# A recurrent cell on one core: one PSUM copy of the odd groups placed ahead of two state copies, split weights made in steps 12 to 19, and DMA waits placed in front of the last store

## The chip, the cores and the metric

The kernel runs on one core of one Trainium2 chip. The metric is the device time of one execution in microseconds (us); the median of three runs of the kernel before is 1650.72 us. The core has five instruction streams that wait for each other through semaphores: TensorE (PE, with its weight loads listed as PEld), VectorE (DVE), ScalarE (ACT), GpSimd (POOL) and SyncE (SP), which issues most DMAs.

## What is computed

x has 8 sequences of 512 steps with 512 features, and h starts from `cond_1024` (8 x 512). Each step needs the state of the step before, so nothing can run ahead along time except the products with x.

```python
def step(h, x_t):
    fused = sigmoid(concatenate([x_t, h], -1) @ w_W + w_b)
    hidden_state, output_state = split(fused, 2, -1)          # r and z
    memory_state = x_t @ wx_W + wx_b + hidden_state * (h @ wh_W + wh_b)
    h_new = output_state * h + (1.0 - output_state) * tanh(memory_state)
    return h_new, h_new
x = x + hs                                                     # hs: all h_new, batch first
```

## The kernel before

**Steps and groups.** The main loop (L615) runs over i = 0 to 511, one time step each. Four steps make a group; eight steps make an octet `o`, and `u` is the step's place in it (L722). Groups with `u` 0 to 3 are called even here, those with `u` 4 to 7 odd. The x side of a whole group is computed ahead, in pieces: behind its own matmuls on h, each step does a share of the products of x for a later group (`x_step`, 384 columns in steps with u 0 to 3 and 288 in the others, L48), and these matmuls write the tiles `xp` and `eps`.

**One step.** The matmuls on h go to three outputs: A (192 columns), B (128) and C (64), in the order of `ORDER` (L26): A0 B0 A1 A2 A3 B1 B2 B3 C0 to C3, where the digit is the quarter of h. C holds the second half of the gate z and lies in the PSUM bank `cs`. DVE transposes the outputs, ACT does sigmoid and tanh, and DVE scans (`m`, then `hT`) make the new state; `hT` of the first half, written by `update(0, 0)` (L726), is what A0 of the next step waits for.

**C in two forms.** In steps where `in_parts(i)` holds (L492: even groups from step 8 on), C is made of bf16 parts: POOL splits h into three parts (`split`, L751 to 761), and 48 bf16 matmuls use the weights `wb`, `w2` and `w3` (`parts`, L434). In the others it is made of 16 f32 matmuls. An f32 matmul of the code stands in the trace as two, so the trace counts 32 where the code has 16. `w2` and `w3` are made by POOL in steps 1 to 4, four operations of 128x128 a step (L762 to 770).

**The x side goes into PSUM ahead of the matmuls.** For an odd group `spread(2 * o + 1, ...)` copies the pieces A, B and C of `odd` into the PSUM banks with ACT: A and C in step u = 1, B in step u = 2 (L795 to 804). C of an odd group lands in the bank `cs`, in which the even group's C is still being made. `spread_c` (L495, four copies with a mask) does it for C of an even group, two in step 6 and two in step 7 (L749).

**ACT around step u = 1.** At a step's end ACT copies the new state into its other slot, a copy for each half (L751). Then, in step u = 1, it copies `eps` to `more` (only for 0 < o < 62, L776 and 797), then `spread` A and C. The next work in its queue is the sigmoid of the next step (`md0A<-tr`).

**What sets the order.** Each engine works through its instructions in the order in which the code adds them. `Flow.plan` (L132) puts a wait in front of an instruction for each operand that another engine still reads or writes; a PSUM bank counts as a whole (L179 to 184), so a matmul into `cs` waits for the last ACT copy into `cs` that the code added before it.

**The end.** In step 511 DVE adds the last half of the output (L855), SP issues the last store (L856), and then SP waits for the semaphores of all 24 DMA lanes (L251 to 253).

Of the kernel before, what the change touches and what calls it, by code (L numbers as in the profile page):

```python
# [11 lines left out]
ALU = mybir.AluOpType  # L12
# [3 lines left out]
NQ = 4  # L16
GS = 4
HS = 12
B = 8
HU = 64  # L20
# [4 lines left out]
IDLE = 3  # L25
# [61 lines left out]
class Flow:  # L87
# [146 lines left out]
    def emit(self, tc):  # L234

        self.plan()
        sems = {e: tc.alloc_semaphore(f"flow_{e}") for e in self.ENGINES}
        lanes = [tc.alloc_semaphore(f"flow_dma{n}") for n in range(self.LANES)]
        count = {}
        with tc.tile_critical():  # L240
            for item in self.items:
                engine = getattr(self.nc, item.engine)
                for other in sorted(item.waits, key=lambda o: o.index):
                    engine.wait_ge(other.sem, other.value)
                inst = getattr(self, item.op, getattr(engine, item.op, None))(*item.args, **item.kw)  # L245
                if item.lane is not None or item.signal:
                    sem, by = (lanes[item.lane], 16) if item.lane is not None else (sems[item.engine], 1)
                    count[sem.name] = count.get(sem.name, 0) + by
                    item.sem, item.value = sem, count[sem.name]
                    inst.then_inc(sem, by)  # L250
            for sem in lanes:  # L251
                if sem.name in count:
                    self.nc.sync.wait_ge(sem, count[sem.name])


@with_exitstack
def tile_cond_rnn_residual(
# [40 lines left out]
    nc = Flow(tc.nc)  # L298
    NCH = x.shape[0]
    T = NCH * TC  # L300
    NG = T // GS
    LAST = NG // 2 - 1
# [56 lines left out]
    wb = const.tile([P, NQ, NQ, 192], F32, name="wb")  # L359
# [13 lines left out]
    NH = 2 * GS  # L373
# [3 lines left out]
    w2 = const.tile([P, NQ, NQ, HU], F32, name="w2")  # L377
    w3 = const.tile([P, NQ, NQ, HU], F32, name="w3")
# [35 lines left out]
    def state(hf, i, slot=2):  # L414

        s = i % GS
        return hT[hf][i % NH][:, B * s : B * s + B, :, slot]
# [13 lines left out]
    def high(t_):  # L431
        return t_.bitcast(BF16)
# [29 lines left out]
    def act(out_, in_, func, **kw):  # L462
        return nc.scalar.activation(out_, in_, func, **kw)
# [10 lines left out]
    def keep(g):  # L474

        nc.vector.tensor_tensor(
            source(g)[:, XC], (piece if g == 2 else xps[g % 2])[:, XC], bias[:, XC], ALU.add
        )

    def source(g):  # L480

        return xps[g % 2] if g // 2 == LAST else (even, odd)[g % 2]

    def spread(g, names):

        for n in names:
            nc.scalar.copy(banks[g % 2][n], source(g)[:, XP[n]])

    def cell(i):
        return cs[:, HU * (i % GS) : HU * (i % GS) + HU] if i // GS % 2 == 0 else banks[1]["C"]  # L490

    def in_parts(i):  # L492
        return NH <= i < T and i // GS % 2 == 0

    def spread_c(g, steps_):  # L495

        for s in steps_:
            nc.scalar.activation(
                cell(GS * g + s), source(g)[:, XP["C"]], AF.Copy, scale=mask[:, s, :1]
            )  # L500

    def turn_x(g, hf):

        c0 = XP["X"].start + HU * hf
        nc.vector.transpose(
            md1[hf][g % 2][:, :, :, 1].rearrange("p n c -> p c n"), source(g)[:, c0 : c0 + HU]
        )

    def reg(r, c=XC):
        return xps[r[0]][r[1], c]  # L510
# [18 lines left out]
    def x_sum(o, n):  # L529

        t_ = [q[o % 2] for q in sx]
        a, b, op = [
            (x_half(o, 1, 0), x_half(o, 1, 1), ALU.add),
            (t_[0], x_half(o, 0, 0), ALU.subtract),
            (x_half(o, 0, 0), x_half(o, 1, 0), ALU.subtract),
            (x_half(o, 0, 1), t_[1], ALU.subtract),
        ][n]
        nc.gpsimd.tensor_tensor(t_[n], a, b, op)
# [76 lines left out]
    for i in range(T):  # L615
# [8 lines left out]
        for n in (ORDER if i else FIRST).split():  # L624
# [3 lines left out]
            bank, k = n[0], int(n[1])  # L628
            lhsT = hs[i % NH][:, k, :32, 2]
            for j in range(NQ):  # L630
                if bank == "C" and in_parts(i):
                    parts(cell(i)[32 * j : 32 * j + 24], i, k, j)
                else:
                    to = cell(i) if bank == "C" else ps[bank]
# [8 lines left out]
        def scan(c_, out_, d0, d1):  # L643

            return nc.vector.tensor_tensor_scan(
                *[t_[:, :, c_].rearrange("p n c s -> p (n c s)") for t_ in (out_, d0, d1)],
                0.0,
                ALU.mult,
                ALU.add,
            ).ins  # L650
# [59 lines left out]
        def update(hf, q):  # L710
            s1 = (i + 1) % GS
            new = hT[hf][(i + 1) % NH][:, B * s1 : B * s1 + B]
            return scan(slice(q, q + 1), new, hd0[hf][i % 2], hT[hf][i % NH][:, rows])
# [8 lines left out]
        o, u = divmod(i, 2 * GS)  # L722
# [22 lines left out]
            memory(1, 1)  # L745
        update(1, 0)
        update(1, 1)
        if nxt and u in (6, 7):
            spread_c(2 * o + 2, (2 * u - 12, 2 * u - 11))  # L749
        for hf in range(2):  # L750
            act(state(hf, i + 1, 0), state(hf, i + 1), AF.Copy)  # L751
            if in_parts(i + 1):
                ks, s1 = slice(2 * hf, 2 * hf + 2), B * ((i + 1) % GS)
                t_, new = split[(i + 1) % 2][:, ks], hs[(i + 1) % NH][:, ks]
                nc.gpsimd.tensor_tensor(
                    t_[:, :, :2].rearrange("p k u b -> p k b u"),
                    new[:, :, s1 : s1 + B, 2].unsqueeze(3).broadcast_to([P, 2, B, 2]),
                    high(new).rearrange("p k (u n) s -> p k n u s", u=2)[:, :, s1 : s1 + B, :, 5],
                    ALU.subtract,
                )  # L760
                nc.gpsimd.tensor_tensor(t_[:, :, 2], t_[:, :, 0], high(t_)[:, :, 0, 1::2], ALU.subtract)
        if 1 <= i <= NQ:  # L762
            for n in range(0, NQ, 2):
                for to, t_ in ((w2, wb[:, :, :, :HU]), (w3, w2)):
                    nc.gpsimd.tensor_tensor(
                        to[:, i - 1, n : n + 2],
                        t_[:, i - 1, n : n + 2],
                        high(t_)[:, i - 1, n : n + 2, 1::2],
                        ALU.subtract,
                    )  # L770
        if i < 3:
            inst = load_x(i + 1)
            if i == 0:
# [5 lines left out]
        if o == LAST:  # L779
            if u == 2:  # L780
                spread(2 * o + 1, "AB")
                turn_x(2 * o + 1, 0)
                turn_x(2 * o + 1, 1)
            elif u == 3:
                spread(2 * o + 1, "C")
        elif u == 0:
            if o == 0:
                spread(1, "A")
            if sums:
                nc.scalar.copy(reg(BE), reg(AL))  # L790
                nc.scalar.copy(both[LO], reg(DE))
                x_sum(o + 1, 3)
            turn_x(2 * o + 1, 0)
            turn_x(2 * o + 1, 1)
        elif u == 1:  # L795
            if sums:
                nc.scalar.copy(more[HI], eps)
            spread(2 * o + 1, "BC" if o == 0 else "AC")
        elif u == 2:
            if sums:  # L800
                nc.vector.tensor_tensor(reg(GA), reg(BE), more[HI], ALU.add)
                nc.scalar.copy(even[LO, XC], reg(AL))
            if o:
                spread(2 * o + 1, "B")
        elif u == 3:
            if sums:
                nc.vector.tensor_tensor(odd[HI, XC], reg(GA), both[LO], ALU.add)
                nc.scalar.copy(both[HI], reg(DE))
            if two:
                x_sum(o + 2, 2)  # L810
        elif u == 4:
            if o == 0:
                keep(3)
            if two:
                nc.scalar.copy(reg(AL), bias[LO, XC])
                x_sum(o + 2, 0)
        elif u == 5:
            if sums:
                nc.vector.tensor_tensor(even[HI, XC], reg(BE), both[HI], ALU.add)
            if two:  # L820
                nc.scalar.copy(reg(DE), step_bias[HI])
        elif u == 6 and nxt:
            spread(2 * o + 2, "AB")
            turn_x(2 * o + 2, 0)
        elif u == 7 and nxt:
            if o:
                nc.scalar.copy(odd[LO, XC], reg(GA))
            turn_x(2 * o + 2, 1)
            if two:
                x_sum(o + 2, 1)  # L830
        if 1 <= i < 9:
            weight_sum(1 if i < 5 else 3, *divmod((i - 1) % 4, 2))
        if i == 2:
            nc.scalar.copy(step_bias[HI], bias[LO, XC])
            nc.gpsimd.tensor_tensor(step_bias[HI], bias[HI, XC], step_bias[HI], ALU.subtract)
        for n in range(IDLE - 1):
            nc.vector.memset(idle[:, n : n + 1], 0.0)
        def add(hf, engine):
            return engine.tensor_tensor(
# [98 lines left out]
```

## Time and profile before

| | |
|---|---|
| three runs, us | 1650.20, 1650.72, 1652.10 |
| the profiled execution: its time, us | 1651.85 |
| its span, first to last instruction, us | 1649.9 |
| granted TensorE clock, mean | 0.999 |
| DVE busy, us | 1241.6 (75%) |
| ACT busy, us | 1256.4 (76%) |
| POOL busy, us | 542.0 (33%) |

The profile has one row for a group of like instructions: the start, the time that they took together, the engine, the line, the operation, what it writes and reads, how many, and in brackets how long the engine sat idle before and what ended that. Nearly all instructions carry the line of the helper that issues them (L245), so groups are told apart by the names of the tiles. A busy PE is no proof that PE is at its peak: the ends of matmuls are modelled, and a matmul that is held up can hide behind the tail of the one before.

### The profile page before, as it was taken

To read this page: it belongs to the slowest core of one execution; us is meant where nothing else is said; L and a number is where in the kernel's file an instruction comes from. 1 tells how busy PE (TensorE), PEld (TensorE's weight loads), DVE (VectorE), ACT (ScalarE), POOL (GpSimd) and SP (SyncE) were. 2 spreads that over 40 slices of the span, in tenths; PEclk is the share of its full clock that TensorE was granted. 3 is DMA by queue.
4 is the path that set the end of the run, shared out by engine and by line. 5 is a ranking of instruction groups with operands and counts; after the bars stand their busy time and mean duration, and the time that the engine had idled before them with its cause. 6 is when DMAs were issued, how large, how long until landed. Compare 5 with 4: busy or idle time off the path is not lost.

```text
span 1649.9 us, 127364 instructions
## 1 busy us (share of the span) xinstructions
PE 1637.8 (99%) x58330; PEld 1394.7 (85%) x50266; DVE 1241.6 (75%) x9443; ACT 1256.4 (76%) x6190; POOL 542.0 (33%) x2304
## 2 busy tenths in 40 slices
PE   8999999999999999999999999999999999999998
PEld 5888888888888888888888888888888888888887
DVE  7777777777777777777777777777777777777776
ACT  4777777777777777777777777777777777777775
POOL 3323323333233233333332333333333333333332
PEclk9999999999999999999999999999999999999999
DMA  4000000000000000000000000000000000000000
GB/s 183 12 15 17 15 15 16 16 15 15 15 17 15 15 15 18 14 15 15 17 15 15 15 18 14 15 15 18 15 14 15 18 15 14 15 18 10 10 10 11
DMA packets 37298, 31.26 MB, mean 19 GB/s; under 512 B 4084, under 2 KB 35060, under 8 KB 36600
## 3 DMA queue, kind: packets, MB, share of 16 engines
q1 hardware_dynamic: 36576, 22.89, 4.5%
q8 instruction: 425, 6.96, 1.7%
q14 instruction: 145, 1.19, 0.2%
q10 hardware_dynamic: 152, 0.22, 0.1%
HBM read 14.70 MB, written 8.39 MB: 14 GB/s over the span
## 4 chain that ended last, share of the span: by engine, by line
PE 98%; DVE 1%; ACT 0%; issue 0%; DVEq 0%; SPq 0%
PE A L245 41%; PE B L245 27%; PE xp L245 17%; PE cs L245 9%; PE cs L219 4%; PE eps L245 1%; DVE m L245 0%; DVE tr L245 0%; DVE tw L245 0%; DVE hT L245 0%; DVE md1A L245 0%; DVE tz L245 0%; DVE md1B L245 0%; DVE even L245 0%; ACT cs L245 0%
## 5 line engine op out<-in xcount | busy, mean ns | idle before, releaser
L245 PE MATMUL A<-wa,hT 128*32 128x192 f32 x16384 | 872.5, 327 | 3.7 <-DVE hT L245 3.7
L245 PEld LDWEIGHTS A<-wa,hT 128*32 128x32 f32 x16384 | 547.9, 122 | 192.8 <-DVE hT L245 134.0
L245 PE MATMUL B<-wb,hT 128*32 128x128 f32 x16384 | 653.1, 273 | 0.0
L245 PEld LDWEIGHTS B<-wb,hT 128*32 128x32 f32 x16384 | 542.8, 122 | 21.2 <-DMA wb<-in_wb_dram 0.9
L245 POOL TENSOR_TENSOR ot<-xin,hT 128x16 f32<-128x16 f32 x991 | 225.4, 252 | 594.4 <-DVE hT L245 592.5
L245 ACT ACTIVATE hT<-m 128x8 f32<-128x8 f32 x2048 | 350.5, 208 | 77.9 <-DVE m L245 68.1
L245 DVE STREAM_TRANSPOSE tr<-A 128x64 f32<-128x64 f32 x512 | 128.2, 250 | 290.1 <-PE A L245 284.0
L245 POOL TENSOR_TENSOR split<-hT 128x32 f32<-128x32 f32 x504 | 131.3, 261 | 432.1 <-DVE m L245 420.3
L245 PE MATMUL xp<-tw,sx 128*32 128x384 f32 (+2 forms) x1464 | 263.4, 433 | 0.0
L245 ACT ACTIVATE hT<-hT 128x16 f32<-128x16 f32 x1024 | 217.0, 225 | 60.3 <-DVE hT L245 57.7
L245 DVE TENSOR_TENSOR_SCAN hT<-hd0B,hT 128x24 f32<-128x24 f32 x1024 | 180.9, 205 | 74.7 <-ACT hT L245 50.7
L245 ACT ACTIVATE md0A<-tr 128x16 f32<-128x16 f32 x512 | 112.2, 219 | 158.1 <-DVE tr L245 156.6
L245 PE MATMUL xp<-wx,xin 128*32 128x384 f32 (+4 forms) x1348 | 220.8, 413 | 0.0
L245 DVE TENSOR_TENSOR_SCAN hT<-hd0A,hT 128x24 f32<-128x24 f32 x1024 | 199.0, 194 | 0.0
L245 PE MATMUL cs<-wb,hT 128*32 128x64 f32 x8320 | 169.3, 219 | 0.0
L245 PEld LDWEIGHTS cs<-wb,hT 128*32 128x32 f32 x8320 | 157.6, 122 | 0.4 <-issue 0.3
L245 DVE TENSOR_TENSOR_SCAN m<-md0A,md1A 128x16 f32<-128x16 f32 x1024 | 143.1, 182 | 16.2 <-ACT md0A L245 8.1
L245 DVE TENSOR_TENSOR_SCAN m<-md0B,md1B 128x16 f32<-128x16 f32 x1024 | 145.6, 163 | 0.8 <-DVE tzB L245 0.4
L219 PE MATMUL cs<-w,split 128*24 128x64 bf16 x8064 | 135.2, 192 | 0.6 <-issue 0.6
L245 ACT ACTIVATE hd0A<-tz 128x16 f32<-128x16 f32 x512 | 115.1, 225 | 18.3
L245 PE MATMUL cs<-wb,split 128*24 128x64 bf16 x4032 | 127.2, 193 | 0.3 <-issue 0.2
L245 PEld LDWEIGHTS cs<-wb,split 128*24 128x24 bf16 x4032 | 108.2, 92 | 21.5 <-issue 12.6
(101 smaller groups left out, 2223.1 us busy)
## 6 DMA issues: line engine op xcount, KB each, us to landing
out_dram<-ot SPq DMA_DIRECT2D x128, 64.0 KB, 1.6
xin<-in_x_dram SPq DMA_DIRECT2D x112, 64.0 KB, 2.4
wx<-in_wx_dram SPq DMA_DIRECT2D x4, 768.0 KB, 7.0
wa<-in_wa_dram SPq DMA_DIRECT2D x4, 384.0 KB, 9.7
wb<-in_wb_dram SPq DMA_DIRECT2D x1, 1152.0 KB, 13.5
xin<-in_x_dram SPq DMA_DIRECT2D x3, 256.0 KB, 3.5
wb<-in_wb_dram SPq DMA_DIRECT2D x1, 384.0 KB, 13.9
head<-in_xh_dram ACTq DMA_DIRECT2D x1, 208.0 KB, 4.7
```

The costliest lines, as they stand in the source:

```text
L219: return t.add_instruction(mybir.InstMatmult(name=self.nc.get_next_instruction_name(), ins=[t.lower_ap(rhs), t.lower_ap(lhsT)], outs=[t.lo ...
L245: inst = getattr(self, item.op, getattr(engine, item.op, None))(*item.args, **item.kw)
```

## The change

- `spread(2 * o + 1, "C")` of step u = 1 is added ahead of the two copies of h, for 0 < o < 63; behind them only A is left. Octet 0 stays as it was.
- `in_parts` begins at step 24 and no longer at step 8: steps 8 to 11 and 16 to 19 make C with f32 matmuls, and their splits of h are gone.
- `w2` and `w3` are made in steps 12 to 19, two operations a step, no longer in steps 1 to 4, four a step.
- Step 511 leaves out its two copies of h and two small memsets on DVE.
- SP waits for all DMA lanes but the last store's ahead of that store, and behind it for that store's alone.

```diff
+            final = self.items[-1]
+            assert final.engine == "sync" and final.lane is not None
+
+            def landed(mine):
+                for lane, sem in enumerate(lanes):
+                    if sem.name in count and (lane == final.lane) == mine:
+                        self.nc.sync.wait_ge(sem, count[sem.name])
+
             for item in self.items:
                 engine = getattr(self.nc, item.engine)
+                if item is final:
+                    landed(False)
...
-            for sem in lanes:
-                if sem.name in count:
-                    self.nc.sync.wait_ge(sem, count[sem.name])
+            landed(True)
...
-        return NH <= i < T and i // GS % 2 == 0
+        return 3 * NH <= i < T and i // GS % 2 == 0
...
+        if 0 < o < LAST and u == 1:
+            spread(2 * o + 1, "C")
         if nxt and u in (6, 7):
             spread_c(2 * o + 2, (2 * u - 12, 2 * u - 11))
-        for hf in range(2):
+        for hf in range(2 if i < T - 1 else 0):
             act(state(hf, i + 1, 0), state(hf, i + 1), AF.Copy)
...
-        if 1 <= i <= NQ:
-            for n in range(0, NQ, 2):
-                for to, t_ in ((w2, wb[:, :, :, :HU]), (w3, w2)):
-                    nc.gpsimd.tensor_tensor(
-                        to[:, i - 1, n : n + 2],
-                        t_[:, i - 1, n : n + 2],
-                        high(t_)[:, i - 1, n : n + 2, 1::2],
-                        ALU.subtract,
-                    )
+        if NH + GS <= i < NH + GS + 2 * NQ:
+            k, n = (i - NH - GS) // 2, slice(i % 2 * 2, i % 2 * 2 + 2)
+            for to, t_ in ((w2, wb[:, :, :, :HU]), (w3, w2)):
+                nc.gpsimd.tensor_tensor(
+                    to[:, k, n], t_[:, k, n], high(t_)[:, k, n, 1::2], ALU.subtract
+                )
...
-            spread(2 * o + 1, "BC" if o == 0 else "AC")
+            spread(2 * o + 1, "BC" if o == 0 else "A")
...
-        for n in range(IDLE - 1):
+        for n in range(IDLE - 1 if i < T - 1 else 0):
             nc.vector.memset(idle[:, n : n + 1], 0.0)
```

First place: ACT's queue at the end of step u = 1 of octet 16 (step 129) of the kernel before, from the last tanh of the step (`hT_68<-m`) to the first sigmoid of the next (`md0A_80<-tr`). `hT_69<-hT_69` are the copies of h, `cs<-odd` is the copy of C.

```order
L245 ACTIVATE hT_68<-m_1_133 128x8 [waits flow_vector]
L245 ACTIVATE hT_69<-hT_69 128x8x2
L245 ACTIVATE hT_69<-hT_69 128x8x2 [waits flow_vector]
L245 COPY more<-eps 64x384
L245 COPY A_118<-odd 128x192
L245 COPY cs<-odd 128x64
L245 ACTIVATE md0A_80<-tr_2_141 128x2x8 [waits flow_vector]
```

The same place of ACT's queue in the changed kernel:

```order
L255 ACTIVATE hT_68<-m_1_133 128x8 [waits flow_vector]
L255 COPY cs<-odd 128x64
L255 ACTIVATE hT_69<-hT_69 128x8x2
L255 ACTIVATE hT_69<-hT_69 128x8x2 [waits flow_vector]
L255 COPY more<-eps 64x384
L255 COPY A_118<-odd 128x192
L255 ACTIVATE md0A_80<-tr_2_141 128x2x8 [waits flow_vector]
```

The copy of C has moved past four instructions, without a wait of its own in either place.

Second place: POOL's queue in steps 12 to 14 of the changed kernel. `ot` are the additions of x to the new state, `w_77` is `w2` and `w_78` is `w3`, `sx` is a sum of x for later products.

```order
L255 TENSOR_TENSOR ot_124<-head,hT_71 128x8x2
L255 TENSOR_TENSOR w_77<-wb 128x128
L255 TENSOR_TENSOR w_78<-w_77 128x128 [waits flow_gpsimd]
L255 TENSOR_TENSOR sx_103<-xin_131 128x64
L255 TENSOR_TENSOR ot_124<-rest,hT_72 128x8x2 [waits flow_vector]
L255 TENSOR_TENSOR ot_124<-rest,hT_72 128x8x2
L255 TENSOR_TENSOR w_77<-wb 128x128
L255 TENSOR_TENSOR w_78<-w_77 128x128 [waits flow_gpsimd]
L255 TENSOR_TENSOR ot_124<-rest,hT_73 128x8x2 [waits flow_vector]
```

In the kernel before such operations stand in POOL's queue in step 1:

```order
L245 TENSOR_TENSOR ot_124<-head,hT_68 128x8x2
L245 TENSOR_TENSOR w_77<-wb 128x128
L245 TENSOR_TENSOR w_78<-w_77 128x128 [waits flow_gpsimd]
L245 TENSOR_TENSOR w_77<-wb 128x128
L245 TENSOR_TENSOR w_78<-w_77 128x128 [waits flow_gpsimd]
L245 TENSOR_TENSOR ot_124<-head,hT_69 128x8x2 [waits flow_vector]
```

Steps 1 to 4 had two pairs each; now steps 12 to 19 have one pair each, and a sum of x of the same step comes behind the pair.

Third place: PE's queue in step 8, from the last matmuls of B on. Before:

```order
L245 MATMUL B_117<-wb,hT_67 32x128 x12
L245 MATMUL cs<-wb,split_75 24x64
L219 MATMUL cs<-w_77,split_75 24x64
L219 MATMUL cs<-w_78,split_75 24x64
L245 MATMUL cs<-wb,split_75 24x64
```

and so on, 48 in all. In the changed kernel:

```order
L255 MATMUL B_117<-wb,hT_67 32x128 x12
L255 MATMUL cs<-wb,hT_67 32x64 x16
L255 MATMUL xp_120<-wx,xin_131 32x384 x2
L255 MATMUL xp_121<-tw_98,sx_102 32x384 x2
L255 MATMUL A_116<-wa,hT_68 32x192 x4
```

The 48 bf16 matmuls of C have become 16 f32 ones; what stands around them is the same.

## The prediction

> **What bounds the kernel now.** The head of the page and the chain that ended last come first:
>
> ```profile
> PE 1637.8 (99%) x58330; PEld 1394.7 (85%) x50266; DVE 1241.6 (75%) x9443; ACT 1256.4 (76%) x6190; POOL 542.0 (33%) x2304
> PE 98%; DVE 1%; ACT 0%; issue 0%; DVEq 0%; SPq 0%
> ```
>
> PE is the bound on paper, with 98% of the chain. But a busy share cannot tell whether PE is held up between two matmuls, so next comes the table of stages, cut at the first A matmul of each step (step 10, the steps 129 and 130, and step 490):
>
> ```profile
> 50.91:54.27 3.36, 3.36 (x125) 2.75 (x93) 2.30 (x20) 2.73 (x13) 1.36 (x6) 1.00 0.03 5
> 428.78:431.96 3.18, 3.18 (x124) 2.57 (x90) 2.52 (x21) 2.70 (x12) 1.66 (x7) 1.00 0.14 38
> 431.96:435.32 3.36, 3.36 (x125) 2.54 (x93) 2.30 (x20) 2.71 (x13) 1.37 (x6) 1.00 0.03 10
> 1575.91:1579.29 3.38, 3.38 (x125) 2.69 (x92) 2.31 (x20) 2.70 (x13) 1.36 (x6) 1.00 0.00 0
> ```
>
> The columns are the stage, its length, and the busy time of PE, PEld, DVE, ACT and POOL. Steps 129 and 130 have the same amount of matmuls on PE, yet step 130, the one with u = 2, takes 3.36 us beside 3.18, and PE looks fully busy in both. Steps 10 and 490, the first and the last of the 61 steps of this kind (octets 1 to 61), show the same. Where the 0.18 us sits is seen in the timeline of steps 129 and 130, weight loads, ACT and DVE:
>
> ```profile
> 430.85 0.47 PEld L245 LDWEIGHTS cs<-wb,split 128*24 128x24 bf16 x16
> 431.71 0.22 DVE L245 STREAM_TRANSPOSE tzB<-cs 128x64 f32<-128x64 f32 x1
> 431.85 0.27 PEld L245 LDWEIGHTS A<-wa,hT 128*32 128x32 f32 x8 [0.39 <-DVE hT L245]
> 431.96 0.52 PE L245 MATMUL A<-wa,hT 128*32 128x192 f32 x8
> 432.47 0.21 ACT L245 ACTIVATE hT<-m 128x8 f32<-128x8 f32 x1
> 432.59 0.22 ACT L245 ACTIVATE hT<-hT 128x16 f32<-128x16 f32 x1
> 432.96 0.23 ACT L245 ACTIVATE hT<-hT 128x16 f32<-128x16 f32 x1 [0.16 <-DVE hT L245]
> 433.21 0.48 ACT L245 COPY more<-eps 64x384 f32<-64x384 f32 x1
> 433.70 0.32 ACT L245 COPY A<-odd 128x192 f32<-128x192 f32 x1
> 433.75 0.25 DVE L245 STREAM_TRANSPOSE tr<-A 128x64 f32<-128x64 f32 x1 [0.81 <-PE A L245]
> 433.95 0.21 ACT L245 COPY cs<-odd 128x64 f32<-128x64 f32 x1
> 434.19 0.22 ACT L245 ACTIVATE md0A<-tr 128x16 f32<-128x16 f32 x1
> 434.28 0.39 PEld L245 LDWEIGHTS cs<-wb,split 128*24 128x24 bf16 x16 [0.20 <-issue]
> ```
>
> In step 129 the weights of C (430.85) follow those of B with no idle time noted. In step 130 (434.28) the load unit sat idle for 0.20 before them, and the ACT copy into the same bank, `cs<-odd`, ends at 434.16. PE waits for that copy. The list of waits has this gap over the whole run:
>
> ```profile
> PEld cs L245 <- issue: 13.0, 65, 0.6
> ```
>
> 65 gaps, 13.0 us, 0.20 each; the view cannot name the releaser ("issue"), the times of the rows above do.
>
> **The change part by part.**
>
> *The copy of C.* It leaves the place at 433.95 and is put between the tanh at 432.47 and the copies of h. The slots there: the first copy of h starts at 432.59, the second waits for DVE until 432.96. The copy of C holds ACT for 0.24 us (433.95 to 434.19); so it runs from 432.59, the first copy of h moves to 432.83, 0.12 later (the step from 432.47 to 432.59) the second could start at 432.95, and it starts at 432.96 as before. `more` and A stay where they are. Nothing waits for the first copy of h before the scans of the next step, 2 us later. The bank is free by then: the last reader of `cs`, a transpose of DVE, ends at 431.93. Gone is PE's wait: C of step 130 starts with B's end. Gone too is the lateness of `md0A`: its input is ready at 434.00 and A lets ACT go at 433.95. What is late next is nothing new: step 130 becomes step 129, in which A0 is ready to load at 431.85 and PE is free at 431.96, so PE itself is the bound. The excess of the steps with u = 2 over their neighbours, from the starts of A0, has a median of 0.162 us over octets 1 to 60; the table above has 0.18 to 0.20 with its rounding, the wait row 0.20 (part of a load's lead is lost, not PE's time). I take 0.163: 61 x 0.163 = **-9.9**, bounds -9 to -13.
>
> *w2 and w3 leave steps 1 to 4.* The stages from step 1 to step 5, and one late step without x on PE:
>
> ```profile
> 21.49:38.30 16.81, 14.67 (x485) 12.37 (x485) 13.94 (x93) 10.46 (x55) 10.44 (x29) 1.00 0.19 54
> 1638.91:1641.99 3.08, 2.84 (x97) 2.50 (x97) 1.93 (x18) 1.73 (x10) 0.45 (x2) 1.00 0.03 5
> 29.87 1.01 POOL L245 TENSOR_TENSOR stepbias<-bias,stepbias 64x384 f32<-64x384 f32 x1 [1.90 <-ACT stepbias L245]
> 30.44 0.58 DVE L245 TENSOR_TENSOR_SCAN m<-md0A,md1A 128x16 f32<-128x16 f32 x2
> 33.93 0.58 DVE L245 TENSOR_TENSOR_SCAN m<-md0A,md1A 128x16 f32<-128x16 f32 x2
> 34.06 0.40 POOL L245 TENSOR_TENSOR w<-wb 128x128 f32<-128x128 f32 x1
> 1641.26 0.28 DVE L245 TENSOR_TENSOR_SCAN m<-md0A,md1A 128x16 f32<-128x16 f32 x2
> ```
>
> Five steps take 16.81, at 3.08 each they would take 15.40: 1.41 too long. The `m` scans take 0.58 beside a POOL operation on `w`, 0.28 alone. Not all of it goes: in step 3 it is `stepbias` that runs beside the scan (29.87 to 30.88), released by ACT and not by the `w` queue, and it stays, 0.30; step 5 keeps an addition of x, some 0.1. So **-1.0**, bounds -0.6 to -1.3.
>
> *w2 and w3 in steps 12 to 19.* By the queue order they start when the additions of the step before are done. Step 13 of the kernel before shows when that is:
>
> ```profile
> 60.55 0.52 PE L245 MATMUL A<-wa,hT 128*32 128x192 f32 x8
> 61.42 0.45 POOL L245 TENSOR_TENSOR ot<-rest,hT 128x16 f32<-128x16 f32 x2 [2.22 <-DVE hT L245]
> ```
>
> The additions end 1.32 after A0 (61.87 less 60.55); the pair takes two times 0.40 and is over 2.2 after A0. The `m` scan starts 2.35 after A0 (1641.26 less 1638.91). So the pair fits in front of the scan; a sum of x behind it (steps 12, 15, 16, 19) does not. I charge 0.1 for each of 12 and 15, none for 16 and 19, whose step is then longer by PE anyway: **+0.2**, bounds 0 to +1.2, what five steps lost to all 16 operations. [...]
>
> *C in f32 in eight steps.* PE from the first matmul of C to the first of `xp`, step 129 and step 132:
>
> ```profile
> 430.96 0.22 PE L245 MATMUL cs<-wb,split 128*24 128x64 bf16 x3
> 431.32 0.49 PE L245 MATMUL xp<-wx,xin 128*32 128x384 f32 x1
> 440.68 0.63 PE L245 MATMUL cs<-wb,hT 128*32 128x64 f32 x32
> 441.12 0.41 PE L245 MATMUL xp<-tw,xin 128*32 128x288 f32 x1
> ```
>
> 0.36 against 0.44, so 0.08 to 0.09 more for f32, and these steps are bound by PE: 8 x 0.087 = **+0.7**, bounds 0 to +0.8. The splits that go away on POOL hide behind PE and bring nothing.
>
> *The end.* The store, and SP's waits behind it:
>
> ```profile
> 1645.86 0.07 DVE L245 MEMSET idle<- 128x1 f32 x2
> 1645.95 0.02 DVEq L244
> 1646.30 0.33 SPq L245 DMA_DIRECT2D out_dram<-ot  x1
> SPq L253 <- DMA out_dram<-ot: 1.0, 1, 1.0
> L253 SPq EVENT_SEMAPHORE  x12: 17/28/28, 1646.7 to 1648.3; - x12
> L240 SPq COMPARE_BRANCH  x1: 38/38/38, 1648.4 to 1648.4; - x1
> ```
>
> From the first wait to the branch it is 1.7, of which 1.0 is the store's landing. The other 0.7 is twelve steps of 0.06, nine of them behind the landing: 0.55. With the others ahead of the store, where SP is idle for some 11 us behind the store before (nothing is queued there but the last store), this saves about 0.55: **-0.55**, bounds -0.4 to -0.6. The two memsets are over before DVE's wait for its own scan (1645.95): 0 to -0.02. The two copies of h at the very end have no reader: 0.
>
> The sum: -9.9 - 1.0 + 0.2 + 0.7 - 0.55 = **-10.6**. The profiled execution took 1651.85 (span 1649.9 and 1.95 around it), which gives 1641.3; it lies 1.1 over the median 1650.72, inside the spread of the runs. From the median it is **1640.1**, my forecast.
>
> **The rivals.**
>
> *The gain is partly lost on ACT.* If the copy of C does not fit into the idle 0.16 ahead of the second copy of h, `more`, A and `md0A` come up to 0.15 late, as now. PE's slack is 431.96 less 431.85, 0.11; 0.04 to 0.05 a step would stay late, 61 x 0.05 = 3: 1643.2. Against it: the slots above add up with 0.01 to spare, and a further 0.09 (433.95 to 434.04) ahead of `md0A`.
>
> *The contention only moves.* The pairs of w slip behind slower additions and meet the scans; at what they cost before, +1.0 in place of +0.2, this gives 1640.9; with a scan held for 0.40 in each of the eight steps +3.2, 1643.1. Against it: the 0.15 between 2.2 and 2.35.
>
> *Another wait takes the place.* C of step 130 is then held by something else, the splits of POOL or `hT`, and only the rest of the sum is left, -0.65: 1650.1. Against it: step 129 has the same splits and no gap.
>
> *Slower.* ACT works in order, so if the copy of C is held at its new place, for the bank `cs` or for `odd`, everything behind it is held: both copies of h, `more`, A and `md0A`. A hold of w us makes `md0A` late by w less 0.10, of which 0.11 is hidden, so a step grows by w - 0.21. The change is slower by 0.2% (3.3 us) once 61 x (w - 0.21) passes 3.3 + 10.6 = 13.9, w = 0.44; with 0.6 it is 61 x 0.39 = 23.8 less 10.6, +13: 1664. Against it: the last reader of `cs` ends at 431.93, 0.66 ahead of 432.59.
>
> **How the numbers follow.** A measurement of this kernel can tell about 0.2%, 3.3 us, from no change. Forecast 0.78, gain partly lost 0.09, contention moves 0.08, another wait 0.03, slower 0.02. The first three are all faster by more than 0.2%: 0.95; same 0.03; slower 0.02. The low end takes the wait row's 13.0 for the main term, half of it believed, and a run at the low side: 1637.3. The high end takes the partly lost gain and a run at the high side: 1643.9.
>
> **What would show it.** In the profile after, steps with u = 2 of octets 1 to 61 take 3.18, like their neighbours; the row of PEld `cs` waiting for issue falls from 65 gaps to about 4; `cs<-odd` stands between the tanh and the copies of h, and the second copy still starts with a wait for DVE. Steps 1 and 2 take near 3.08, step 3 still 3.4. Steps 8 to 11 and 16 to 19 take about 3.27. `m` scans of 0.28 in steps 13 and 14 show the pairs of w out of the way. The branch behind the store follows its landing at once. Steps with u = 2 that stay over 3.25 would prove the main step wrong.

## The result, and the profile after

| | before | after |
|---|---|---|
| median of five runs on one chip, us | 1652.01 | 1637.78 |
| lowest and highest of them, us | 1650.2, 1652.99 | 1637.59, 1640.49 |
| ratio after to before, 95% interval | | 0.992 (0.991 to 0.9931) |
| span of the profiled execution, us | 1649.9 | 1635.5 |

The changed kernel is faster by 0.8%, 13.2 us by the ratio (11.4 to 14.9). The forecast was 10.6 us less. The page after has the same bound on paper, PE, and one row of the list of waits for the weights of C, where before had a second one with 65 gaps:

```profile
PE 1625.4 (99%) x58202; PEld 1397.4 (85%) x50394; DVE 1235.8 (76%) x9433; ACT 1254.0 (77%) x6188; POOL 531.8 (33%) x2272
PEld cs L255 <- DVE none L255: 2.3, 1, 2.3
```

The row "PEld cs <- issue" is gone; the wait that is left is one at the start of the run. The stages of the changed kernel, with the columns of the table of before (length; busy time of PE, PEld, DVE, ACT, POOL; clock), are step 129, steps 130 and 490 (u = 2), then steps 1 to 5 together, step 3 of them alone, steps 12 to 15 together and step 16:

```profile
425.63:428.81 3.18, 3.18 (x124) 2.50 (x91) 2.52 (x21) 2.70 (x12) 1.64 (x7) 1.00 0.14 36
428.81:432.01 3.20, 3.20 (x126) 2.47 (x94) 2.23 (x18) 2.70 (x13) 1.35 (x6) 1.00 0.03 8
1562.38:1565.55 3.17, 3.17 (x124) 2.46 (x91) 2.26 (x20) 2.69 (x13) 1.35 (x6) 1.00 0.02 8
...
21.80:37.54 15.74, 14.45 (x485) 12.49 (x485) 12.63 (x93) 10.13 (x55) 4.24 (x13) 1.00 0.17 58
27.96:31.38 3.42, 2.84 (x97) 2.50 (x97) 2.72 (x19) 2.25 (x11) 1.56 (x4) 1.00 0.02 7
56.83:69.26 12.43, 12.43 (x436) 11.67 (x432) 8.94 (x71) 9.04 (x47) 5.37 (x18) 1.00 0.04 11
69.26:72.53 3.27, 3.27 (x109) 2.91 (x109) 2.24 (x22) 2.67 (x14) 1.48 (x5) 1.00 0.15 43
```

Step 130 is now as long as step 129 and step 490 as its neighbours. PE looked fully busy in the long steps of before, too: the wait could be read from the length of the stage, not from PE's busy share. The timeline around step 130 shows ACT, the load unit and DVE in the new order:

```profile
428.69 0.27 PEld L255 LDWEIGHTS A<-wa,hT 128*32 128x32 f32 x8 [0.39 <-DVE hT L255]
429.31 0.21 ACT L255 ACTIVATE hT<-m 128x8 f32<-128x8 f32 x1
429.55 0.22 ACT L255 COPY cs<-odd 128x64 f32<-128x64 f32 x1
429.70 0.35 ACT L255 ACTIVATE hT<-hT 128x16 f32<-128x16 f32 x2
430.06 0.47 ACT L255 COPY more<-eps 64x384 f32<-64x384 f32 x1
430.44 0.32 ACT L255 COPY A<-odd 128x192 f32<-128x192 f32 x1
430.59 0.25 DVE L255 STREAM_TRANSPOSE tr<-A 128x64 f32<-128x64 f32 x1 [0.81 <-PE A L255]
430.87 0.22 ACT L255 ACTIVATE md0A<-tr 128x16 f32<-128x16 f32 x1
430.88 0.46 PEld L255 LDWEIGHTS cs<-wb,split 128*24 128x24 bf16 x16
```

The copy of C (429.55) starts 0.24 behind the tanh (429.31). The weights of C (430.88) follow with no idle time, and `md0A` starts as soon as its input is there (430.59 and 0.25 make 430.84).

**Where the time went.** The starts of the first A matmul of each step cut the run into lengths. Of the 58 octets 3 to 60, a median for each u is taken; u = 2 falls from 3.344 to 3.187 us, and all others stay within 0.01. What a step takes beyond the median of its kind is counted apart, as late steps.

| stretch, us | before | after | difference |
|---|---|---|---|
| steps 1 to 5 | 16.80 | 15.74 | -1.06 |
| steps 8 to 23 | 50.66 | 50.98 | +0.32 |
| steps 24 to 487, 58 times the eight medians | 1468.33 | 1459.02 | -9.31 |
| steps 488 to 510 | 72.43 | 72.20 | -0.23 |
| from A0 of step 511 to the end of the span | 7.93 | 7.30 | -0.63 |
| sum of these | | | -10.9 |
| late steps, 24 to 487 | 6.0 | 2.2 | -3.8 |
| ahead of A0 of step 0 | 15.36 | 15.66 | +0.30 |

The first five rows recur: in the second trace of each kernel, told below, each of the two sums is within 0.4 of the one here. Their difference, -10.9, is close to the forecast. The +0.32 of steps 8 to 23 is the price of C in f32 less what steps 10 and 18, which have u = 2, win. The last row scatters between 15.1 and 16.3 over all traces, whatever the kernel. The late steps were not in the forecast at all. They, and the surplus of the measured 13.2 over 10.9, were the open question of the experiments.

### The profile page after: what moved, and what is told of

The parts are those of the page before. It is cut to its first block, busy times and chain, and to the rows that moved or that the text cites. A ratio compares the mean times of both kernels' runs of the same rounds, so it can differ in the third digit from the quotient of the medians.

```text
span 1635.5 us, 127307 instructions
## 1 busy us (share of the span) xinstructions
PE 1625.4 (99%) x58202; PEld 1397.4 (85%) x50394; DVE 1235.8 (76%) x9433; ACT 1254.0 (77%) x6188; POOL 531.8 (33%) x2272
## 3 DMA queue, kind: packets, MB, share of 16 engines
q8 instruction: 425, 6.96, 1.7%
q14 instruction: 144, 1.18, 0.2%
## 4 chain that ended last, share of the span: by engine, by line
PE 98%; DVE 1%; DMA 0%; ACT 0%; issue 0%; DVEq 0%; ACTq 0%; SPq 0%
PE A L255 41%; PE B L255 27%; PE xp L255 17%; PE cs L255 9%; PE cs L219 4%; PE eps L255 1%; DMA head<-in_xh_dram 0%; DVE tr L255 0%; DVE m L255 0%; DVE tw L255 0%; DVE hT L255 0%; DVE md1A L255 0%; DVE tz L255 0%; DVE md1B L255 0%; DVE even L255 0%
## 5 line engine op out<-in xcount | busy, mean ns | idle before, releaser
L255 POOL TENSOR_TENSOR split<-hT 128x32 f32<-128x32 f32 x488 | 126.0, 258 | 410.0 <-DVE m L255 397.9
L255 ACT ACTIVATE hT<-hT 128x16 f32<-128x16 f32 x1022 | 210.3, 225 | 50.1 <-DVE hT L255 47.8
L255 PE MATMUL cs<-wb,hT 128*32 128x64 f32 x8576 | 173.0, 219 | 0.0
L255 PEld LDWEIGHTS cs<-wb,hT 128*32 128x32 f32 x8576 | 161.4, 122 | 0.0
L219 PE MATMUL cs<-w,split 128*24 128x64 bf16 x7808 | 129.9, 192 | 0.0
L255 PE MATMUL cs<-wb,split 128*24 128x64 bf16 x3904 | 122.2, 192 | 0.0
L255 POOL TENSOR_TENSOR split<-split 128x16 f32<-128x16 f32 x488 | 105.2, 216 | 38.2
```

Of the source, the lines that this page charges most:

```text
L219: return t.add_instruction(mybir.InstMatmult(name=self.nc.get_next_instruction_name(), ins=[t.lower_ap(rhs), t.lower_ap(lhsT)], outs=[t.lo ...
```

## The experiments

Each kernel ran in several rounds beside the kernel before; the kernels of one group ran on one chip. "Gain" is the median of before times one less the ratio. "u = 2" is the median of the steps with u = 2, "late" the sum of the late steps, both from the profiled execution.

| label | us | ratio (95%) | gain, us | u = 2, us | late, us |
|---|---|---|---|---|---|
| `c_alone` | 1644.17 | 0.9934 (0.9921 to 0.9946) | 10.9 | 3.186 | 6.8 |
| `c_alone_2` | 1645.27 | 0.9924 (0.991 to 0.9937) | 12.6 | 3.188 | 8.0 |
| `c_undone` | 1652.33 | 0.9987 (0.9978 to 0.9995) | 2.2 | 3.342 | 5.6 |
| `c_undone_2` | 1653.86 | 0.9979 (0.997 to 0.9987) | 3.5 | 3.340 | 9.0 |
| `c_between` | 1646.01 | 0.9947 (0.9933 to 0.996) | 8.8 | 3.187 | 3.3 |
| `after_again` | 1640.78 | 0.9912 (0.9899 to 0.9926) | 14.6 | 3.186 | 6.9 |
| `before_again` | 1656.29 | 0.9995 (0.9984 to 1.0005) | 0.8 | 3.345 | 10.6 |
| `w_four` | 1642.04 | 0.9909 (0.9895 to 0.9923) | 15.1 | 3.187 | 6.6 |
| `waits_back` | 1642.10 | 0.9905 (0.9892 to 0.9919) | 15.7 | 3.186 | 6.5 |
| `best` | 1640.36 | 0.9903 (0.989 to 0.9917) | 16.1 | 3.185 | 4.4 |
| `after_shift64` | 1641.51 | 0.9911 (0.9897 to 0.9924) | 14.8 | 3.187 | 6.0 |
| `best_dve75` | 1641.53 | 0.9905 (0.9892 to 0.9919) | 15.7 | 3.185 | 5.7 |

The median of before was 1655.25, 1657.47 and 1657.6 in the three groups of runs, so only ratios compare across them.

### The copy of C alone, and everything but it

The kernel before, with the copy of C moved and nothing else:

```diff
+        if 0 < o < LAST and u == 1:
+            spread(2 * o + 1, "C")
         if nxt and u in (6, 7):
...
-            spread(2 * o + 1, "BC" if o == 0 else "AC")
+            spread(2 * o + 1, "BC" if o == 0 else "A")
```

> The kernel before with the copy of C moved ahead of the copies of h and nothing else changed. Theory 1 (PE waits for the copy of C; strays, i.e. single steps that are late by 0.1 to 0.6 us, depend on the layout and are not part of the edit): steps with u = 2 fall from 3.34 to 3.18-3.19, the sum over 61 steps is 9.6 to 9.9 us, and the time is 9 to 10 us below the kernel before, give or take 2 for strays. Theory 2 (the early copy also takes the strays away, because they hit steps in which ACT was the late engine): 12 to 13 us below, with the excess of late steps down from 6 us to about 2.

The changed kernel, with the copy of C back behind A:

```diff
-        if 0 < o < LAST and u == 1:
-            spread(2 * o + 1, "C")
...
-            spread(2 * o + 1, "BC" if o == 0 else "A")
+            spread(2 * o + 1, "BC" if o == 0 else "AC")
```

> The changed kernel with the copy of C put back behind A, all else as changed. Theory 1 (strays depend on the layout): steps with u = 2 are at 3.34 again, 9.6 us in all; the time is 9 to 10 us above the changed kernel give or take 2. Theory 2 (strays come with the late copy): 12 to 13 us above the changed kernel, with about 6 us of late steps.

The copy alone gives 10.9 us of gain, with 6.8 us of late steps, as its Theory 1 has it. The other edits alone give 2.2, and that kernel is 11.6 slower than the changed kernel of the same group (1640.78), between the 9 to 10 and the 12 to 13 of its two theories. Together the two parts are 13.1; the change as a whole gave 13.2 in the first comparison and 14.6 in this group (`after_again`). With the copy back, the list of waits has its row again:

```profile
PEld cs L255 <- issue: 12.0, 60, 0.4
```

60 gaps of 0.20. So PE's wait for the bank `cs` is made by the place of this one copy and by nothing else in the change. The stretches of the table above that recur in every execution differ from before by -9.7 us for the copy alone and by -1.3 for the rest; each gain is about 1 us larger than that. The two were run again for this surplus:

> A second run of the kernel before with the copy of C moved alone. The step lengths give 9.7 us for it; the first comparison had 10.9 (ratio 0.9934, 0.9921 to 0.9946). Theory (the surplus over the step lengths is a matter of single steps held up by chance, differing from execution to execution): ratio 0.9934 to 0.9945 again, with single late steps of 3 to 10 us in all at other places. Rival (moving the copy itself takes single late steps away): the ratio stays at or under 0.9934 and the sum of the late steps lies at least 2 us below that of the kernel before.

> A second run of the changed kernel with the copy of C back behind A: the other edits alone, which the step lengths put at 1.3 us together. Theory (surplus by chance): ratio 0.9987 to 0.9996. Rival (the other edits take single late steps away): ratio about 0.998, 3 us or more.

By the ratio both came out on the rival's side, 12.6 and 3.5 us, though both intervals still touch the theories' ranges. The surplus was there a second time, so luck in one run is unlikely to be all of it. The sum of late steps cannot carry the proof, though: it is 8.0 for `c_alone_2`, and it scatters from execution to execution of the same kernel, 6.0 and 10.6 for before. So the late steps were sorted by what is late first in them; this is told below.

### The copy of C behind the copies of h

```diff
-        if 0 < o < LAST and u == 1:
-            spread(2 * o + 1, "C")
         if nxt and u in (6, 7):
...
                 nc.gpsimd.tensor_tensor(t_[:, :, 2], t_[:, :, 0], high(t_)[:, :, 0, 1::2], ALU.subtract)
+        if 0 < o < LAST and u == 1:
+            spread(2 * o + 1, "C")
```

> The changed kernel with the copy of C behind both copies of h and ahead of more. PE then has its bank before it gets to C, but more, A and the sigmoid of the next step are as late as in the kernel before (0.15 us). Theory 1 (the PE wait made the excess, the late sigmoid hides in PE's slack of 0.11): steps with u = 2 take 3.18 to 3.24, the time is 0 to 3 us above the changed kernel. Rival (the late sigmoid made the excess): 3.34, 9.6 us above it.

It fits neither expectation as put: u = 2 falls in full, to 3.187, but the steps with u = 3 grow, by 0.115 at the median (3.292). The stages of the steps 146 and 147 and the timeline from step 146 into step 147 of this kernel show how:

```profile
481.43:484.61 3.18, 3.18 (x125) 2.33 (x90) 2.15 (x19) 2.71 (x13) 1.36 (x6) 1.00 0.02 5
484.61:487.90 3.29, 3.29 (x125) 2.47 (x92) 2.98 (x22) 2.51 (x12) 1.63 (x7) 1.00 0.02 5
...
482.67 0.22 ACT L255 COPY cs<-odd 128x64 f32<-128x64 f32 x1
482.91 0.47 ACT L255 COPY more<-eps 64x384 f32<-64x384 f32 x1
483.29 0.32 ACT L255 COPY A<-odd 128x192 f32<-128x192 f32 x1
483.61 0.22 ACT L255 ACTIVATE md0A<-tr 128x16 f32<-128x16 f32 x1
484.60 0.19 PEld L255 LDWEIGHTS A<-wa,hT 128*32 128x32 f32 x8 [0.50 <-DVE hT L255]
484.61 0.54 PE L255 MATMUL A<-wa,hT 128*32 128x192 f32 x8
485.55 0.51 PEld L255 LDWEIGHTS A<-wa,hT 128*32 128x32 f32 x16 [0.20 <-DVE hT L255]
```

Here are the same rows of the changed kernel, steps 146 and 147:

```profile
479.38:482.57 3.19, 3.19 (x124) 2.61 (x92) 2.29 (x20) 2.69 (x13) 1.36 (x6) 1.00 0.02 5
482.57:485.75 3.18, 3.18 (x124) 2.54 (x89) 2.85 (x21) 2.51 (x12) 1.62 (x7) 1.00 0.02 5
...
481.45 0.22 ACT L255 ACTIVATE md0A<-tr 128x16 f32<-128x16 f32 x1
482.43 0.29 PEld L255 LDWEIGHTS A<-wa,hT 128*32 128x32 f32 x8 [0.36 <-DVE hT L255]
482.57 0.51 PE L255 MATMUL A<-wa,hT 128*32 128x192 f32 x8
483.01 0.91 PEld L255 LDWEIGHTS A<-wa,hT 128*32 128x32 f32 x24
```

`md0A` starts 2.18 after A0 in place of 2.07. In step 146 this lateness is hidden, because the load of A0 was 0.14 ahead of PE (482.43 and 482.57); now it is level with it (484.60 and 484.61). The second half of h is as late as the first, and it has no such lead: in step 147 the weight loads of A stop for 0.20 to wait for it (485.55), where the changed kernel loads all 24 without a stop (483.01). Step 147 pays 0.11. So the 0.14 that protected the start of A0 in step 146 protected that one start only. Over the 58 octets this makes 6.6 us, and the time is 5.2 over the changed kernel beside it.

### More weight operations in a step

Four operations of `w2` and `w3` a step in steps 12 to 15, in place of two a step in steps 12 to 19:

```diff
-        if NH + GS <= i < NH + GS + 2 * NQ:
-            k, n = (i - NH - GS) // 2, slice(i % 2 * 2, i % 2 * 2 + 2)
-            for to, t_ in ((w2, wb[:, :, :, :HU]), (w3, w2)):
...
+        if NH + GS <= i < NH + GS + NQ:
+            k = i - NH - GS
+            for n in (slice(0, 2), slice(2, 4)):
+                for to, t_ in ((w2, wb[:, :, :, :HU]), (w3, w2)):
```

> The changed kernel with w2 and w3 made four operations a step in steps 12 to 15 in place of two a step in 12 to 19. Theory 1 (an operation on w costs where it runs beside an m or hT scan): the second pair runs from 2.2 to 3.0 us after A0, over the m scan at 2.3 and the hT scan at 2.8, so the m scans go from 0.28 to 0.4-0.6 us and steps 12 to 15 are each 0.1 to 0.4 longer, 0.5 to 1.4 us in all. Rival (it cost in steps 1 to 4 only because those steps have other work on DVE and POOL): steps 12 to 15 stay at 3.105-3.11.

Steps 12 to 16 take 0.17 us more in all than in the changed kernel, less than expected, but not nothing. In step 13, two rows each of POOL and DVE show the reason, first with four operations and then, in the changed kernel, with two:

```profile
61.71 0.40 POOL L255 TENSOR_TENSOR w<-wb 128x128 f32<-128x128 f32 x1
61.89 0.35 DVE L255 TENSOR_TENSOR_SCAN m<-md0A,md1A 128x16 f32<-128x16 f32 x2
```

```profile
61.69 0.40 POOL L255 TENSOR_TENSOR w<-w 128x128 f32<-128x128 f32 x1
62.24 0.28 DVE L255 TENSOR_TENSOR_SCAN m<-md0A,md1A 128x16 f32<-128x16 f32 x2
```

A scan pair that begins in the middle of a POOL operation (61.89, in 61.71 to 62.11) takes 0.35, not 0.28; in the changed kernel the scan starts behind POOL's end (62.24 and 62.09) and takes 0.28. The scan was neither held back until POOL had ended nor for the 0.40 of a whole operation.

### The waits behind the last store

All the waits of SP stand behind the store again, the last store's own as the last of them:

```diff
-                if item is final:
-                    landed(False)
...
+            landed(False)
             landed(True)
```

> The changed kernel with SP's waits for the 24 DMA lanes all behind the last store again; nothing else changes. Theory: the end of the span, from A0 of step 511, is 0.55 to 0.63 us longer than in the changed kernel (7.30), at 7.85 to 7.95, with some nine waits of 0.06 us between the landing and the branch; the ratio to the kernel before 0.0004 higher, which the time cannot tell. Rival (the waits cost nothing at the end and the shorter tail comes from the two copies of h and the memsets left out): the tail stays at 7.30.

The tail is 7.37, not 7.85: neither theory. The rows of SP, first of this kernel and then of the changed one, are the issue of the store, the waits with their first and last start, and the branch behind them:

```profile
1637.29 0.33 SPq L253 DMA_DIRECT2D out_dram<-ot  x1
L247 SPq EVENT_SEMAPHORE  x12: 17/28/28, 1637.7 to 1638.8; - x12
L240 SPq COMPARE_BRANCH  x1: 38/38/38, 1638.9 to 1638.9; - x1
```

```profile
1632.53 0.33 SPq L255 DMA_DIRECT2D out_dram<-ot  x1
L247 SPq EVENT_SEMAPHORE  x10: 28/28/28, 1620.9 to 1622.6; - x10
L240 SPq COMPARE_BRANCH  x1: 38/38/38, 1634.1 to 1634.1; - x1
```

From the issue to the branch it is 1.6 in both, and 2.1 in before (1646.30 and 1648.4 in the prediction's rows). The store is issued 4.31 us after A0 of step 511 in all three, so the two copies of h and the memsets that step 511 leaves out are not what shortened the tail. The eleven other waits cost nothing here, since they pass while the store is landing. In before, nine stood behind the wait for the store, in order of lane number. So the edit's gain is that the last store's wait comes last; that the others stand ahead of the store is worth 0.07. This kernel was a poor test of the expectation, which overlooked that its waits did not go back into the old order.

### Steps 3 and 507

The forecast named `stepbias` in step 3 as what stays. This version makes it ahead of the loop, and moves the last group's turning of x from step 506 to 507:

```diff
+            nc.scalar.copy(step_bias[HI], bias[LO, XC])
+            nc.gpsimd.tensor_tensor(step_bias[HI], bias[HI, XC], step_bias[HI], ALU.subtract)
     keep(0)
...
+            elif u == 3:
                 turn_x(2 * o + 1, 0)
                 turn_x(2 * o + 1, 1)
-            elif u == 3:
...
-        if i == 2:
-            nc.scalar.copy(step_bias[HI], bias[LO, XC])
-            nc.gpsimd.tensor_tensor(step_bias[HI], bias[HI, XC], step_bias[HI], ALU.subtract)
```

> The changed kernel with two more moves: the subtraction that makes stepbias stands ahead of the loop and no longer in step 2, and the two transposes of x for the last group stand in step 507 and no longer in 506. Theory: the m scan of step 3 falls from 0.5 to 0.19 us and step 3 from 3.42 to 3.08-3.12 us; step 507 falls from 3.33 to 3.16. In all 0.5 us less than the changed kernel, below what the times can tell. Rival: step 3 keeps its length (the subtraction was not the cause), or the prologue grows by up to 0.6 us.

Step 3 of this kernel, to be held against the 3.42 of the changed kernel above:

```profile
28.19:31.26 3.07, 2.84 (x96) 2.49 (x96) 2.38 (x19) 1.72 (x10) 0.95 (x3) 1.00 0.03 8
```

0.35 goes there, and step 507 falls from 3.33 to 3.17. Whether the time ahead of the loop grew cannot be told: A0 of step 0 starts at 15.9 here, and at 15.7 and 15.1 in the two traces of the changed kernel. Its ratio of 0.9903 is the lowest of all runs, but a gain of 0.5 over the changed kernel is less than the intervals can tell.

### The late steps: what repeats without a change, and two shifts of instructions

Both kernels ran again unchanged, for the spread:

> The changed kernel once more, unchanged. [...]

> The kernel before once more. Over the stages that do not vary (steps 1 to 511 less their late steps, and the end) the traces so far give 10.9 us between the two kernels, the times 14. Theory 1 (the rest is late steps of the first trace): ACT's late steps 42, 137, 164, 259 and 449 stand again, and the sum of late steps is 6 to 9 us, 2 to 4 above the changed kernel's mean. Rival (chance): 2 to 6 us, no more than the changed kernel has.

The first trace after was a lucky one: its late steps, 27, 36, 131, 152 and 321 above all, are 2.2 us in all, against 6.9 in the second, and 27 and 152 are not late again. The second trace of before has 10.6, more than either side of its expectation allowed. But some places recur. Steps 36, 131 and 321 are late by 0.22 to 0.25 in every trace of the changed kernel, and 42, 137, 164, 259 and 449 in both of before. To see whose queue sets these places, 64 tiny copies were added to ACT's queue in the prologue:

```diff
+    pad = const.tile([P, 64], F32, name="pad")
+    for n in range(64):
+        nc.scalar.copy(pad[:, n : n + 1], zeros[:, :1])
```

> The changed kernel with 64 tiny copies more on ACT ahead of the first step, where ACT waits for data anyway. [...] Late steps in which PE stops in the middle of a row of matmuls stay where they were (39, 343, 344, 351, 399, 407). Rival: 36, 131 and 321 stay late. The time is the changed kernel's within 2 us.

36, 131 and 321 stayed: the theory that ACT's queue sets them fell. Of the six steps in which PE had stopped, 39, 344 and 399 were late again, and 343, 351 and 407 were not. What is late first in 36, 131 and 321 is a scan of DVE, and each of them is an instruction of DVE whose number, counted from the start with DVE's semaphore waits, leaves 63 when divided by 128. So 75 tiny memsets were added to DVE's queue, in the version of the last section:

```diff
     idle = const.tile([P, IDLE], F32, name="idle")
+    pad = const.tile([P, 75], F32, name="pad")
+    for n in range(75):
+        nc.vector.memset(pad[:, n : n + 1], 0.0)
```

> The version with the stepbias subtraction ahead of the loop, with 75 tiny memsets more on DVE in the prologue; nothing that a step computes changes. Theory (DVE's own queue): in the traces of the changed kernel, every 128th instruction of DVE starts 0.265 us late where DVE would otherwise go straight on, which is between tzB<-cs and m<-md0B and around the tzs reduce. So 75 instructions more move the late steps from 36, 131 and 321 to 65, 160, 187, 282 and 472 (and 500 and 507 in the last octets), each 0.2 to 0.25 us longer than the median of its kind: about 0.9 us more in all, less than the time can tell, so the trace decides. Rival (a fixed place in time or in PE's queue): 36, 131 and 321 stay late and the new ones are not.

36, 131 and 321 are no longer late, and the five named instructions are. The trace lists them in steps 66, 161, 188, 283 and 473, one further than named, because they stand just ahead of A0 and their lateness carries them past it. The two named for the last octets are late too: step 500 takes 3.41 and not 3.16, step 507 3.35 and not 3.17. DVE at step 131 and then at step 66, with the 75 memsets:

```profile
432.51 0.23 DVE L255 STREAM_TRANSPOSE tzB<-cs 128x64 f32<-128x64 f32 x1
432.66 0.16 DVE L255 TENSOR_TENSOR_SCAN m<-md0B,md1B 128x16 f32<-128x16 f32 x1
...
226.93 0.23 DVE L255 STREAM_TRANSPOSE tzB<-cs 128x64 f32<-128x64 f32 x1
227.34 0.19 DVE L255 TENSOR_TENSOR_SCAN m<-md0B,md1B 128x16 f32<-128x16 f32 x1 [0.18 <-issue]
```

The scan follows its transpose by 0.15 at step 131 and by 0.41 at step 66. Without the memsets, in the version of the last section, it is the other way round (step 131, then step 66):

```profile
433.12 0.22 DVE L255 STREAM_TRANSPOSE tzB<-cs 128x64 f32<-128x64 f32 x1
433.56 0.19 DVE L255 TENSOR_TENSOR_SCAN m<-md0B,md1B 128x16 f32<-128x16 f32 x1 [0.21 <-issue]
...
226.81 0.22 DVE L255 STREAM_TRANSPOSE tzB<-cs 128x64 f32<-128x64 f32 x1
226.96 0.15 DVE L255 TENSOR_TENSOR_SCAN m<-md0B,md1B 128x16 f32<-128x16 f32 x1
```

So these late steps belong to the places of DVE's instructions in its own stream. The change as a whole has two such steps fewer, 0.70 in place of 1.13 us: 0.4 of the surplus.

The other late steps begin on PE, in the middle of a row of matmuls. Step 179 of before is 0.58 too long; its C matmuls:

```profile
589.99 0.22 PE L219 MATMUL cs<-w,split 128*24 128x64 bf16 x2
590.63 0.19 PE L219 MATMUL cs<-w,split 128*24 128x64 bf16 x1 [0.42 <-issue]
```

These stops lie at one place of PE's stream: of the 11 of over 0.08 in the first trace of before that stand in steps with all their rows, outside the first rows of a step, each is at an instruction of PE's queue (matmuls, weight loads and the semaphore waits between them) whose number leaves 193 or 194 when divided by 256. The page's queues fit this, here those of the changed kernel:

```profile
q8 instruction: 425, 6.96, 1.7%
q14 instruction: 144, 1.18, 0.2%
```

425 packets of 16 KB (6.96 MB by 425) for 108,596 rows of PE and PEld and some 200 waits are one for every 256. DVE's places are 128 apart, and the packets of q14 are 8 KB (1.18 MB by 144). No view names the engine that a queue serves: that q8 is PE's is the author's estimate from this count, and that the packets make the stops was not shown.

Sorted by step, the stops of over 0.05 that fall among the C matmuls of the steps with u = 2 and 3 go with the place of the copy of C. They are 1.7, 3.2, 1.4 and 2.5 us in the four traces that have it behind A (`before`, `before_again`, `c_undone`, `c_undone_2`), and 0.1 to 0.5, 0.3 in the mean, in the nine with the copy ahead of the copies of h; all 13 have 32 or 33 of the places that leave 193 or 194 there. (`c_between`, with the copy behind the copies of h and ahead of A, is left out of these sums; it has one such stop, of 0.1.) Thus some 1.9 us more go with the copy, or 1.7 if only the lateness at these very places is added up. In the steps of the other kinds such stops do not sort by the copy: 1.3 to 3.4 us with it behind A, 0.1 to 4.1 with it ahead. The sorting was done after the runs, and no run was made to test it. Why a stop is more likely there with the copy behind A isn't known. It isn't that PE has less time between two such places: for those in u = 3 it is about 3.75 us with the copy behind A, and about 3.6 with it ahead.

## Why the prediction was right, and where it was off

**PE waited for the copy of C: right.** The steps with u = 2 fell by 0.157 in place of 0.163, 61 times that is 9.6 for 9.9; with the copy alone as with all edits, and its return brings the wait back. The excess of the step lengths was the right measure; the 13.0 us of the row of waits, the far bound, are more than the steps gave back.

**The slots on ACT: wrong, without harm.** The prediction put the copy of C 0.12 behind the tanh and left the second copy of h, `more` and A in their places. The copy of C started 0.24 behind it, and the second copy of h no longer waits for DVE but starts 0.03 later. Its margin of 0.09 ahead of `md0A` was wrong as well: it let ACT go 0.25 behind the start of A (433.70 to 433.95), which is the step to another copy, while the sigmoid follows A by 0.32 where ACT is late (483.29 to 483.61 in `c_between`). By the prediction's slots ACT would have been free at 434.02, level with the input at 434.00. `md0A` is in time all the same, as the rows after show: A starts 0.38 behind `more` (430.06 to 430.44), and not 0.49 as before (433.21 to 433.70), so ACT is free at some 430.76, ahead of the input at 430.84. Why A follows `more` sooner is not known.

**The price of what stays late on ACT: mis-sized.** The rival "partly lost on ACT" charged lateness less a slack of 0.11 in A0. `c_between` shows that a lateness of 0.11 costs 0.115: the slack hides it in one step, and the next step pays by the second half of h. The rival didn't come about, but its term, 0.05 a step, was wrong.

**w2 and w3 out of steps 1 to 4: right.** 1.06 for 1.0, and step 3 keeps its 3.42 because of `stepbias`, as the version that moves it shows. Step 5, which was to keep 0.1 for an addition of x, keeps nothing (3.08), and step 3 keeps 0.34 for the 0.30: two small errors that cancel in part.

**w2 and w3 in steps 12 to 19: too dear.** Charged at 0.2, they cost nothing: the steps 12 to 15 take 12.43, as they did before (57.44 to 69.87), and 16 to 19 take 3.265 each, like 8 to 11, which have no pair. The rival by which each of the eight steps holds a scan for 0.40 would have given 3.2, but no run shows a scan held for the 0.40 of a whole POOL operation: four operations a step, with scans beside them, cost 0.17 in all, and the scan pair in step 13 took 0.35 there and not 0.28.

**C in f32: right.** The eight steps take 3.265 beside 3.18, 8 times 0.085 is 0.7.

**The end: right in size, 0.63 for 0.55, and the reason half right.** The waits behind the landing were the cost; but the cure is their order, not their place ahead of the store.

**What wasn't in the sum.** The recurring stretches give -10.9 for the forecast's -10.6. The first trace had 3.8 us fewer late steps, and five rounds of runs gave 13.2 for the change, 14.6 for its repeat. Of this surplus, 0.4 are the late places of DVE and 1.7 to 1.9 the stops of PE in the steps with u = 2 and 3, together 2.1 to 2.3; with the recurring 10.9 that makes 13.0 to 13.2. That this meets the measured 13.2 so closely is luck: the four traces with the copy behind A differ by 1.8 in these stops, and the interval of the measured gain is 11.4 to 14.9. For the gains of 14.6 to 15.7 in the later groups, whose before had 10.6 us of late steps where it was profiled, 1 to 2.5 us stay unaccounted for. The prediction took one profiled execution as the kernel's time and did not ask which part of it recurs.

## What to carry to other kernels

When an engine waits for a bank, look first for the last writer that stands in that bank's queue and is ready early: here its place among ACT's copies cost PE 0.157 us in a step with u = 2, and moving one line got it back. Follow a lateness for two steps: in `c_between` the slack at the start of step 146 hid 0.11 in that step, and step 147 paid 0.11. Put a wait that ends last in the last place, and let the others pass in its shadow: with that order the tail is 7.37 in `waits_back` and was 7.93 before.

## What the runs showed of the hardware that was not expected

- DVE started about 0.26 us late at places 128 instructions apart in its stream, where it would have gone straight on (a scan 0.41 behind its transpose and not 0.15). 75 instructions more moved the places as counted.
- PE stopped at places 256 instructions apart in its queue (for 0.42 in step 179 of before, which took 0.58 more than its kind), in some executions and not in others at the same place.
- The ACT copy of `odd` into PSUM started 0.24 after the tanh ahead of it (429.31 to 429.55), the copy of h within SBUF that stood there before 0.12 after it (432.47 to 432.59). The two differ in the kind of instruction as well (COPY and ACTIVATE). Neither the destination nor the kind accounts for it alone: in the trace of before the COPY `A<-even` into PSUM starts 0.12 after the copy of h ahead of it in all 61 steps that have the two, and the ACTIVATE `cs<-even,mask` into PSUM 0.10 after the tanh ahead of it. What makes the difference is open.
- A DVE scan pair beside POOL operations took 0.40, 0.49, 0.58 and 0.58 in steps 1 to 4 of before (in step 3 beside `stepbias`), but 0.35 in step 13 of `w_four`, where it began in the middle of one operation, and 0.28 in the same step of the changed kernel, where it began behind POOL's end.
